# Attention sums of the last 14 row blocks in four column-group passes instead of two, with plain sums in the GRU state

## The chip, the cores and the metric

The kernel runs on one core of a Trainium2 chip as one launch. Its time is the device time of that launch in microseconds (us). The engines of the core work side by side and wait for each other by semaphores: TensorE (PE, matrix products; its weight loads are listed as PEld), VectorE (DVE), ScalarE (ACT, functions such as sigmoid and tanh), GpSimd (POOL), and SyncE (SP), which only issues transfers (DMA). A matrix product reads on-chip memory (SBUF) and writes one of eight banks of the accumulation memory (PSUM), where it can be added to what is there; the other engines read the banks.

## The reference, cut to what matters

The program is a graph network of four layers on 3327 nodes with 64 features each. Each layer is `x = x + L(relu(layernorm(x)), adj)`, with `adj` a matrix of 3327 x 3327 zeros and ones (about 0.5% ones). Layers 0 and 3 are hyperbolic attention layers; layer 1 is a decayed sum over neighbours. The change lies in layer 2:

```python
def gru_cell(x, h, w_ih, w_hh, b_ih, b_hh):
    gi = x @ w_ih.T + b_ih
    gh = h @ w_hh.T + b_hh
    ir, iz, inn = jnp.split(gi, 3, axis=1)
    hr, hz, hn = jnp.split(gh, 3, axis=1)
    r = jax.nn.sigmoid(ir + hr)
    z = jax.nn.sigmoid(iz + hz)
    n = jnp.tanh(inn + r * hn)
    return (1.0 - z) * n + z * h
...
A_node = node_adj - jnp.diag(d_node)
A_edge = edge_adj - jnp.diag(d_edge)
node_support = jnp.concatenate([(A_node > 0).astype(h.dtype) @ h, (A_node < 0).astype(h.dtype) @ h], axis=1)
edge_output = gru_cell(node_support, h, w_ih_e, w_hh_e, b_ih_e, b_hh_e)
edge_support = gat(h, A_node, A_edge, W_gat, a_gat)
node_output = gru_cell(edge_support, h, w_ih_n, w_hh_n, b_ih_n, b_hh_n)
return d_edge[:, None] * edge_output + d_node[:, None] * node_output
```

Since no entry of `adj` is negative, and all entries that count are one, every softmax in `gat` is the same over a row's neighbours: the attention is their mean. So layer 2 needs one product, the sum of h over each node's neighbours without the node itself (`A @ h`), and from it two GRU cells: g = 0 with the sum as its input, g = 1 with the mean (sum divided by degree) times W_gat. Only nodes with an entry on the diagonal of `adj` use the result.

## The kernel before, in words

**Layout.** The 3328 (padded) nodes are 26 row blocks of 128 (T = 26). Layer 2 works transposed: features on the 128 partitions, nodes along the columns; partitions 0 to 63 hold the features of the first 1664 nodes (half o = 0), partitions 64 to 127 those of the other half (HP = 1664). The columns of a half are C = 4 groups of BK = 416[...]. `masks` holds the whole adjacency as 8-bit ones and zeros with a cleared diagonal, `parts` the layer's h as a sum of two 16-bit halves.

**Sums.** `block(n, ks)` (L1761) adds row block n into the banks of the column groups ks: 2 parts x 2 halves = 4 matmuls per group (L1767). Group k's sum lies in bank k. Banks 0 and 1 are one PSUM tile, as are 2 and 3, 4 and 5, 6 and 7; a reader of one bank of a tile is ordered by the framework's tracking of tiles. The main loop (L1847) runs blocks 3 to 25; blocks up to 11 (`FULL` = 12) do all four groups, 16 matmuls, and blocks 12 to 25 only groups 0 and 1, 8 matmuls. Groups 2 and 3 of blocks 12 to 25 are done later.

**Small work inside the main loop.** `todo` (L1843) hangs work behind some blocks: `degrees` (L1779) corrects the degree of one column group by the diagonal (matmuls L1775, subtraction L1781); `inverse` (L1831) takes 1/degree by logarithm and exponential on ScalarE (L1834, L1835, L1836), and then loads ScalarE's table for sigmoid and tanh (L132); `inverse2` (L1839) refines it by two DVE operations over all 1664 columns; `weights2` (L1803) transposes W_gat and copies it (`wgT`), `weights3` (L1808) multiplies it into the weights of cell 1 (matmul L1811, copy L1812); `turn` (L1814) transposes up to four blocks of h (L1819) and makes five copies (on ACT L1827, on DVE L1825) into `hP` and the lower or upper half of the four tiles `xh[g][o]`.

**Eight steps.** A step (g, k) is one GRU cell on one column group. For each: `take` (L1869) copies the group's sum from its bank into xh[0] (ACT), `mean` (L1878) makes the mean from the bank and 1/degree (DVE), `take2` (L1882) copies that into xh[1] (ACT); `products` (L1887) are 16 matmuls into four banks (L1894 for r and z, 8 in all; L1899 for the two parts of n, 8); `sigmoids` (L1901) makes the two gates on ACT; `before_tanh` (L1909) combines the n parts on DVE (L1914, L1915); `tanh` (L1917) is on ACT; `state` (L1920) combines on DVE into `oP`, three operations for g = 0 and four for g = 1, which adds to the result of g = 0. The loop L1964 to the end is software pipelined by one step: in turn u come products(u), sigmoids(u), tanh(u−1), before_tanh(u), take2, state(u−1). Each engine has its own queue and runs its instructions in exactly this order; an instruction that waits holds up all behind it on its engine.

The order of steps is (0,0), (0,1), (1,0), (1,1), then (0,2), (0,3), (1,2), (1,3). The sums of groups 2 and 3 for blocks 12 to 25 stand between: 4, 3, 3, 3 and 1 blocks of 8 matmuls ahead of products(0) to products(4). Then the takes and means of groups 2 and 3. The four banks of products rotate over three pairs of banks (`RING`, L1861).

**The end of the stage.** The result goes back to node-major layout by transposes on PE (`turned`, L1943), and `use` (L1938) multiplies by the diagonal and adds to X on DVE (L1940, L1941). Tiles 0 to 5 go by plain transposes (L1271, in `from_pairs`). For tiles 6 to 12 the last two steps (1,2) and (1,3) don't add into `oP`: they leave two summands in two side tiles (`to_sum`; `state` L1926, L1927, cleared by GpSimd at L1867 where a tile of 128 crosses the group's edge), and PE adds the three terms by three matmuls with the identity per tile in PSUM (L1951). `last` is called at u = 6 (tiles 0 to 5), 7 (6 to 8) and 8 (9 to 12). Behind it layer 3 begins with the layernorm's reduction over the whole X (L434).

Of the kernel before, what the change touches and what calls it, by code (L numbers as in the profile page):

```python
# [10 lines left out]
F32 = mybir.dt.float32  # L11
# [10 lines left out]
P = 128  # L22
# [26 lines left out]
def tile_gnn4(ctx: ExitStack, tc: tile.TileContext, x, adjT, att0, b0, w1, bias1, w_gat, a_gat,  # L49
# [1694 lines left out]
    def plain_gat(masks, zo, deg, first, wg, gru, H, parts, banks, last_x, finish, close):  # L1744
# [9 lines left out]
        with ExitStack() as st:  # L1754
# [24 lines left out]
            def degrees(k, to):  # L1779
                cs = slice(k * BK, (k + 1) * BK)  # L1780
                V.tensor_sub(deg[:, cs], deg[:, cs], diagonal(k, to))  # L1781
# [18 lines left out]
            for _ in range(1):  # L1800
# [38 lines left out]
                def inverse2():  # L1839
                    V.scalar_tensor_tensor(deg, deg, -1.0, r0, op0=OP.mult, op1=OP.mult)  # L1840
                    V.scalar_tensor_tensor(deg, deg, 2.0, r0, op0=OP.add, op1=OP.mult)

                todo = {3: lambda: (degrees(2, 4), weights2(6)), 10: lambda: (degrees(3, 5), inverse()),  # L1843
                        12: lambda: turn(0, 6), 16: lambda: (inverse2(), turn(4, 4, V)),
                        22: lambda: weights3(7), 23: lambda: turn(8, 6), 25: lambda: turn(12, 5)}
                V.tensor_scalar(zo[:, 2 * T:2 * T + 2], zo[:, 2 * T:2 * T + 2], first, None, op0=OP.mult)
                for n in range(3, T):  # L1847
                    block(n, range(C) if n < FULL else range(C // 2))
                    if n in todo:
                        todo[n]()  # L1850
# [6 lines left out]
                halves = range(C // 2), range(C // 2, C)  # L1857
                steps = [(g, k) for ks in halves for g in range(2) for k in ks]
                K = len(steps)
                pg, gates, nns = {}, {}, {}  # L1860
                RING = 2, 3, 0  # L1861
                groups = range(0, 4), range(4, 6), range(6, 9), range(9, C2)
                c6 = groups[2].start * P
                summed = [(1, k) for k in halves[1]]
                to_sum = [tp.tile([P, HP - c6], F32, name=f"sum{i}") for i in range(2)]
                for t in to_sum:
                    G.memset(t[:, :C // 2 * BK - c6], 0.0)  # L1867

# [18 lines left out]
                def products(u):  # L1887
                    g, k = steps[u]
                    cs = slice(k * BK, (k + 1) * BK)
                    wx = gru[g][0]  # L1890
                    pg[u] = pr, pz, ph, pi = [bank(2 * RING[(2 * u + i // 2) % 3] + i % 2)[:, :BK] for i in range(4)]
                    for i, to in enumerate((pr, pz)):
                        for o in range(2):
                            PE.matmul(to[o * D:(o + 1) * D, :], wx[:, i, :], xh[g][o][:, cs], start=True, stop=True)  # L1894
                    for o in range(2):

                        for to, q in ((pi, o), (ph, 1 - o)):
                            r = slice(0, D) if to is pi else slice(D, P)
                            PE.matmul(to[q * D:(q + 1) * D, :], wx[r, 2, :], xh[g][q][r, cs], start=True, stop=True)  # L1899
# [9 lines left out]
                def before_tanh(u):  # L1909
                    bt = gru[steps[u][0]][1]  # L1910
                    g, k = steps[u]
                    nn = nns[u] = (to_sum[0][:, k * BK - c6:(k + 1) * BK - c6] if (g, k) in summed else
                                   tp.tile([P, BK], F32, name="nn", bufs=3))
# [6 lines left out]
                def state(u):  # L1920
# [3 lines left out]
                    if (g, k) in summed:  # L1924
                        o = to_sum[1][:, k * BK - c6:(k + 1) * BK - c6]
                        V.tensor_sub(o, hP[:, cs], nn)  # L1926
                        V.tensor_mul(o, o, gates[u][1])  # L1927
                        return
# [14 lines left out]
                def turned(i):  # L1943
                    pt = banks[2 + i % 2].rearrange("p (t h d) -> p t h d", h=2, d=D)
                    if i < 2:
                        from_pairs(None, oP, lambda *a: None, None, groups[i], pt)
                    else:
                        for k, t in enumerate(groups[i]):
                            for j in range(3):
                                src = oP[:, t * P:(t + 1) * P] if j == 0 else to_sum[j - 1][:, t * P - c6:(t + 1) * P - c6]  # L1950
                                PE.matmul(pt[:, k, :, :], src, ident, start=j == 0, stop=j == 2)  # L1951
                    return pt[:, :len(groups[i])].rearrange("p t h d -> p h t d")

                def last(*i):
                    for i, pt in [(i, turned(i)) for i in i]:
                        use(groups[i].start, len(groups[i]), pt)

                def takes(ks):
                    take(ks[0])
                    for k in ks:  # L1960
                        mean(k)
                    take(ks[1])

                blocks = iter(range(FULL, T))  # L1964
                between = {0: 4, 1: 3, 2: 3, 3: 3, 4: 1}
                takes(halves[0])
                for u in range(K + 2):
                    for _ in range(between.get(u, 0)):
                        block(next(blocks), halves[1])
                    if u == 4:  # L1970
                        takes(halves[1])
# [11 lines left out]
                    last(*{6: (0, 1), 7: (2,), 8: (3,)}.get(u, ()))  # L1983
# [103 lines left out]
```

## Time and profile before

| | |
|---|---|
| three timed executions | 731.65, 735.44, 739.38 us (median 735.44) |
| profiled execution | 731.25 us, span 729.4 us, mean granted TensorE clock 0.964 |
| busy share of the span | PE 87%, PEld 36%, DVE 74%, ACT 73%, POOL 59% |
| layer 2's sums and cells, up to L434's start | 380.8 to 466.8 us: 86.0 us |
| of it the main loop, up to the first products | 380.8 to 418.4 us |
| the eight steps' products | 418.4 to 449.0 us |
| the rest of the stage | 449.0 to 466.8 us |
| layer 3 | 466.8 to 729.4 us |

How to read it: all times are from one execution, counted from the start of its span. A row of the timeline has start, duration, engine, line of the source, operation, output and input by the program's names, shape and type, count of instructions in the row, and in brackets the engine's idle time before it with what ended it. The windows give each engine's busy time in a stretch, the number of its instructions, and the clock that TensorE was granted (1.00 is full). Matrix products are pipelined: a single one is listed with the time it takes from start to end, though the next begins earlier; the length of a stream is read from the starts.

### The profile page before, as it was taken

To read this page: it belongs to the slowest core of one execution; us is meant where nothing else is said; L and a number is where in the kernel's file an instruction comes from. 1 tells how busy PE (TensorE), PEld (TensorE's weight loads), DVE (VectorE), ACT (ScalarE), POOL (GpSimd) and SP (SyncE) were. 2 spreads that over 40 slices of the span, in tenths; PEclk is the share of its full clock that TensorE was granted. 3 is DMA by queue.
4 is the path that set the end of the run, shared out by engine and by line. 5 is a ranking of instruction groups with operands and counts; after the bars stand their busy time and mean duration, and the time that the engine had idled before them with its cause. 6 is when DMAs were issued, how large, how long until landed. Compare 5 with 4: busy or idle time off the path is not lost.

```text
span 729.4 us, 12038 instructions
## 1 busy us (share of the span) xinstructions
PE 638.0 (87%) x4262; PEld 261.9 (36%) x4262; DVE 541.9 (74%) x998; ACT 534.3 (73%) x688; POOL 430.0 (59%) x328
## 2 busy tenths in 40 slices
PE   0799999999999798989999996469999999999940
PEld 0522233333333233444446542442223333333310
DVE  6867777777777799999645458596667877777756
ACT  2788888888888785777861855258888889888831
POOL 2699989999999102017520000048887787888820
PEclk9999999999999999999999998569999999999985
DMA  3998888998888716489930000203334344433001
GB/s 63 325 280 277 265 276 257 284 289 269 265 262 270 254 56 224 134 290 359 402 130 2 1 1 1 93 18 94 95 93 133 107 118 144 119 118 118 2 2 50
DMA packets 61494, 119.25 MB, mean 164 GB/s; under 512 B 9552, under 2 KB 33776, under 8 KB 61424
## 3 DMA queue, kind: packets, MB, share of 16 engines
q1 hardware_dynamic: 57072, 118.38, 50.3%
q10 hardware_dynamic: 4352, 0.02, 0.3%
q8 instruction: 35, 0.57, 0.3%
q14 instruction: 35, 0.29, 0.1%
HBM read 115.64 MB, written 0.88 MB: 160 GB/s over the span
## 4 chain that ended last, share of the span: by engine, by line
PE 62%; DVE 13%; ACT 9%; issue 5%; POOL 5%; DMA 3%; ACTq 1%; SPq 0%; POOLq 0%; DVEq 0%
PE slot L630 16%; PE slot L638 9%; PE slot L611 9%; PE slot L1467 8%; PE slot L612 7%; PE slot L1481 5%; POOL sig L600 5%; PE slot L1767 3%; DMA adj<-in 3%; ACT sig L598 2%; PE slot L1894 1%; ACT slot L617 1%; PE slot L1951 1%; DVE X L1520 1%; ACTq L307 1%
## 5 line engine op out<-in xcount | busy, mean ns | idle before, releaser
L621 DVE SCALAR_TENSOR_TENSOR sig<-slot,sig 128x768 f32<-128x768 f32 (+1 forms) x208 | 212.5, 1022 | 106.4 <-POOL sig L600 106.1
L617 ACT ACTIVATE slot<-slot 128x768 f32<-128x768 f32 (+1 forms) x208 | 177.2, 852 | 54.1 <-PE slot L612 53.9
L600 POOL TENSOR_TENSOR sig<-adj,sig 128x768 f32<-128x768 f32 (+1 forms) x104 | 201.2, 1960 | 13.6 <-ACT sig L598 8.8
L598 ACT ACTIVATE sig<-leftB,right 128x768 f32<-128x768 f32 (+1 forms) x208 | 203.1, 977 | 0.1
L600 POOL TENSOR_TENSOR sig<-mask,sig 128x768 f32<-128x768 fp8e4 (+1 forms) x104 | 173.3, 1679 | 40.3 <-ACT sig L598 35.0
L630 PE MATMUL slot<-sig,Xr 128*64 128x384 f32 (+1 forms) x832 | 169.5, 526 | 6.3 <-DVE sig L621 6.1
L611 PE MATMUL slot<-XC,XT 128*128 128x384 f16 (+1 forms) x416 | 142.2, 342 | 2.9 <-ACT sum L648 1.7
L612 PE MATMUL slot<-XF,XE 73*128 73x384 f16 (+1 forms) x416 | 141.4, 340 | 0.0
L638 PE MATMUL slot<-sig,X 128*32 128x384 f32 (+1 forms) x832 | 94.2, 525 | 0.0
L1473 ACT ACTIVATE w<-slot,ebias 128x832 bf16<-128x832 f32 x76 | 69.0, 951 | 26.3 <-PE slot L1467 25.9
L630 PEld LDWEIGHTS slot<-sig,Xr 128*64 128x64 f32 x832 | 49.7, 135 | 87.9 <-issue 61.8
L611 PEld LDWEIGHTS <-XT 128*128 128x128 f16 x416 | 40.6, 98 | 93.8 <-issue 67.4
L1467 PE MATMUL slot<-mask,rest 128*128 128x416 fp8e4 x208 | 53.9, 341 | 5.7 <-ACT adj L1473 3.5
L1467 PE MATMUL slot<-mask,after 128*128 128x416 fp8e4 x208 | 53.4, 339 | 1.3 <-DVE deg L1491 1.3
L612 PEld LDWEIGHTS <-XE 73*128 73x128 f16 x416 | 40.7, 98 | 29.3 <-issue 5.1
L1362 DVE TENSOR_SCALAR_CACHE_REDUCE same<-late 128x832 fp8e4<-128x832 f32 x48 | 48.4, 1008 | 0.0
L204 POOL TENSOR_TENSOR mask<-mask,offdiag 128x128 fp8e4<-128x128 fp8e4 x26 | 15.4, 603 | 47.4 <-PE slot L1467 46.1
L638 PEld LDWEIGHTS slot<-sig,X 128*32 128x32 f32 x832 | 16.4, 108 | 67.7 <-issue 66.1
L1767 PE MATMUL slot<-mask,own 128*64 128x416 fp8e4 x416 | 39.4, 340 | 0.4 <-DVE deg L1491 0.4
L527 PE MATMUL pt<-ident_h,Xp 128*64 128x128 f16 x32 | 2.6, 314 | 36.1 <-ACT Xp L466 36.1
L1481 PE MATMUL slot<-w,h 128*64 128x416 bf16 x304 | 34.0, 345 | 0.0
L1512 POOL TENSOR_TENSOR X<-X,bias 128x256 f32<-128x256 f32 (+1 forms) x7 | 5.3, 785 | 46.1 <-DVE Xr L1527 46.1
(334 smaller groups left out, 690.6 us busy)
## 6 DMA issues: line engine op xcount, KB each, us to landing
adj<-in SPq DMA_DIRECT2D x78, 384.0 KB, 4.4
late<-in SPq DMA_DIRECT2D x48, 416.0 KB, 3.2
adj<-in SPq DMA_DIRECT2D x17, 832.0 KB, 8.0
adj<-in SPq DMA_DIRECT2D x27, 512.0 KB, 5.1
ahead<-in SPq DMA_DIRECT2D x14, 832.0 KB, 5.9
ahead<-in SPq DMA_DIRECT2D x16, 416.0 KB, 4.8
own<-in SPq DMA_DIRECT2D x16, 416.0 KB
own<-in SPq DMA_DIRECT2D x8, 832.0 KB
```

The costliest lines, as they stand in the source:

```text
L598: A.activation(sig, leftB[c], AF.Sigmoid, bias=right[:, b:b + 1])
L600: G.tensor_tensor(sig, adj, sig, op=OP.mult)
L611: PE.matmul(L[:, o, :c[1] * P], XT[:, rows], XC[c][:, o, :], start=True, stop=False)
L612: PE.matmul(L[:, o, :c[1] * P], XE[:KE, rows], XF[c][:, o, :], start=False, stop=True)
L617: A.activation(L, L, AF.Arctan, scale=PA / SX ** 2)
L621: V.scalar_tensor_tensor(sig, slot[:, :, :tiles[k][0][1] * P], PC, sig, op0=OP.add, op1=OP.mult)
L630: PE.matmul(acc[c][o * D:(o + 1) * D, 0, :n], Xr[:, b, :], sigs[k][:, o, :], start=b == 0, stop=b == T - 1)
L638: PE.matmul(acc[c][q:q + 32, 1, :n], X0[:, b - 1 + i, :], w[:, o, :], start=b == 1, stop=b == T - 1, tile_position=(0, q))
L1467: PE.matmul(cnt[o][:, h, :BK], w, cols(k, o, h), start=w is after and steps[k][1] == T - 1, stop=True, skip_group_check=True)
L1473: A.activation(ws[k][:, o, :, :], cnt[o][:, :, :BK], AF.Exp, scale=-LN2, bias=ebias)
L1481: PE.matmul(acc[c][o * D:(o + 1) * D, h, :BK], parts[i][:, b, :], w[:, o, h, :], start=b == T - 1 and i == 0, stop=b == 0 and i == 1)
L1767: PE.matmul(acc[k][o * D:(o + 1) * D, :], w, mask[:, o * HP + k * BK:o * HP + (k + 1) * BK], start=n == 0 and i == 0, stop=n == T - 1 and ...
```

## The change

The main loop's blocks 12 to 25 do group 0 alone (4 matmuls). The steps are ordered by group: (0,0), (1,0), (0,1), (1,1), (0,2), (1,2), (0,3), (1,3). Ahead of products(u), for u = 0 to 5, seven of the blocks 12 to 25 (the even ones at even u, the odd ones at odd u) are done for group u//2 + 1, 28 matmuls; so group 1 is summed during the two steps of group 0, group 2 during those of group 1, group 3 during those of group 2. At even u follow the take and the mean of group u//2. The side tiles, their memsets and the three-term sums are gone: every state adds into `oP`, and every tile goes back by a plain transpose, in groups of 3, 3, 3 and 4 tiles at u = 3, 5, 7 and 8, by way of banks 0 and 1. Products use banks 4 to 7 in every step but u = 6, which uses 2, 3, 0 and 1. In the main loop, turn(0), degrees(3) with inverse, weights2, inverse2 (now in two halves of 832 columns), weights3 and turn(8) hang behind other blocks; turn(12) stands in step 0 behind the take.

```diff
--- before.py
+++ after.py
@@ -1836,16 +1836,17 @@
                     A.activation(r0, r0, AF.Exp, scale=-1.0)
                     table_of(AF.Sigmoid, r0[:, :1])
-                def inverse2():
-                    V.scalar_tensor_tensor(deg, deg, -1.0, r0, op0=OP.mult, op1=OP.mult)
-                    V.scalar_tensor_tensor(deg, deg, 2.0, r0, op0=OP.add, op1=OP.mult)
-
-                todo = {3: lambda: (degrees(2, 4), weights2(6)), 10: lambda: (degrees(3, 5), inverse()),
-                        12: lambda: turn(0, 6), 16: lambda: (inverse2(), turn(4, 4, V)),
-                        22: lambda: weights3(7), 23: lambda: turn(8, 6), 25: lambda: turn(12, 5)}
+                def inverse2(c):
+                    d, r = [t[:, c * CW:(c + 1) * CW] for t in (deg, r0)]
+                    V.scalar_tensor_tensor(d, d, -1.0, r, op0=OP.mult, op1=OP.mult)
+                    V.scalar_tensor_tensor(d, d, 2.0, r, op0=OP.add, op1=OP.mult)
+
+                todo = {3: lambda: (degrees(2, 4), turn(0, 6)), 9: lambda: (degrees(3, 5), inverse()),
+                        11: lambda: weights2(7), 14: lambda: inverse2(0), 16: lambda: turn(4, 4, V),
+                        19: lambda: (weights3(6), inverse2(1)), 21: lambda: turn(8, 7)}
                 V.tensor_scalar(zo[:, 2 * T:2 * T + 2], zo[:, 2 * T:2 * T + 2], first, None, op0=OP.mult)
                 for n in range(3, T):
-                    block(n, range(C) if n < FULL else range(C // 2))
+                    block(n, range(C if n < FULL else 1))
                     if n in todo:
                         todo[n]()
@@ -1854,18 +1855,9 @@
-                halves = range(C // 2), range(C // 2, C)
-                steps = [(g, k) for ks in halves for g in range(2) for k in ks]
+                steps = [(g, k) for k in range(C) for g in range(2)]
                 K = len(steps)
                 pg, gates, nns = {}, {}, {}
-                RING = 2, 3, 0
-                groups = range(0, 4), range(4, 6), range(6, 9), range(9, C2)
-                c6 = groups[2].start * P
-                summed = [(1, k) for k in halves[1]]
-                to_sum = [tp.tile([P, HP - c6], F32, name=f"sum{i}") for i in range(2)]
-                for t in to_sum:
-                    G.memset(t[:, :C // 2 * BK - c6], 0.0)
-
                 def take(k, on=A):
                     cs = slice(k * BK, (k + 1) * BK)
                     for o in range(2):
@@ -1888,7 +1880,7 @@
                     g, k = steps[u]
                     cs = slice(k * BK, (k + 1) * BK)
                     wx = gru[g][0]
-                    pg[u] = pr, pz, ph, pi = [bank(2 * RING[(2 * u + i // 2) % 3] + i % 2)[:, :BK] for i in range(4)]
+                    pg[u] = pr, pz, ph, pi = [bank(i)[:, :BK] for i in ((2, 3, 0, 1) if u == K - 2 else range(4, 8))]
                     for i, to in enumerate((pr, pz)):
                         for o in range(2):
                             PE.matmul(to[o * D:(o + 1) * D, :], wx[:, i, :], xh[g][o][:, cs], start=True, stop=True)
@@ -1908,9 +1900,7 @@
                 def before_tanh(u):
                     bt = gru[steps[u][0]][1]
-                    g, k = steps[u]
-                    nn = nns[u] = (to_sum[0][:, k * BK - c6:(k + 1) * BK - c6] if (g, k) in summed else
-                                   tp.tile([P, BK], F32, name="nn", bufs=3))
+                    nn = nns[u] = tp.tile([P, BK], F32, name="nn", bufs=3)
                     V.scalar_tensor_tensor(nn, pg[u][2], bt[:, 5:6], gates[u][0], op0=OP.add, op1=OP.mult)
                     V.tensor_add(nn, nn, pg[u][3])
@@ -1921,11 +1911,6 @@
                     g, k = steps[u]
                     cs = slice(k * BK, (k + 1) * BK)
                     nn = nns[u]
-                    if (g, k) in summed:
-                        o = to_sum[1][:, k * BK - c6:(k + 1) * BK - c6]
-                        V.tensor_sub(o, hP[:, cs], nn)
-                        V.tensor_mul(o, o, gates[u][1])
-                        return
                     o = tp.tile([P, BK], F32, name="o", bufs=1)
                     V.tensor_sub(o, hP[:, cs], nn)
                     if g == 1:
@@ -1940,35 +1925,22 @@
                     V.tensor_mul(o[:, :, :n, :], src, d2[:, :, t0:t0 + n, None].to_broadcast([P, 2, n, D]))
                     V.tensor_add(X2[:, :, t0:t0 + n, :], X2[:, :, t0:t0 + n, :], o[:, :, :n, :])
-                def turned(i):
-                    pt = banks[2 + i % 2].rearrange("p (t h d) -> p t h d", h=2, d=D)
-                    if i < 2:
-                        from_pairs(None, oP, lambda *a: None, None, groups[i], pt)
-                    else:
-                        for k, t in enumerate(groups[i]):
-                            for j in range(3):
-                                src = oP[:, t * P:(t + 1) * P] if j == 0 else to_sum[j - 1][:, t * P - c6:(t + 1) * P - c6]
-                                PE.matmul(pt[:, k, :, :], src, ident, start=j == 0, stop=j == 2)
-                    return pt[:, :len(groups[i])].rearrange("p t h d -> p h t d")
-
-                def last(*i):
-                    for i, pt in [(i, turned(i)) for i in i]:
-                        use(groups[i].start, len(groups[i]), pt)
-
-                def takes(ks):
-                    take(ks[0])
-                    for k in ks:
-                        mean(k)
-                    take(ks[1])
-
-                blocks = iter(range(FULL, T))
-                between = {0: 4, 1: 3, 2: 3, 3: 3, 4: 1}
-                takes(halves[0])
+                groups = range(0, 3), range(3, 6), range(6, 9), range(9, C2)
+
+                def last(i):
+                    from_pairs(None, oP, use, None, groups[i],
+                               banks[i % 2].rearrange("p (t h d) -> p t h d", h=2, d=D))
+
                 for u in range(K + 2):
-                    for _ in range(between.get(u, 0)):
-                        block(next(blocks), halves[1])
-                    if u == 4:
-                        takes(halves[1])
+                    k = u // 2 + 1
+                    for n in range(FULL, T):
+                        if k < C and n % 2 == u % 2:
+                            block(n, range(k, k + 1))
+                    if u % 2 == 0 and u < K:
+                        take(u // 2)
+                        mean(u // 2)
+                    if u == 0:
+                        turn(12, 7)
                     if u < K:
                         products(u)
                         sigmoids(u)
@@ -1980,7 +1952,8 @@
                         take2(steps[u][1])
                     if 0 <= u - 1 < K:
                         state(u - 1)
-                    last(*{6: (0, 1), 7: (2,), 8: (3,)}.get(u, ()))
+                    if u in (3, 5, 7, 8):
+                        last((3, 5, 7, 8).index(u))
     def load():
         for ts in HALVES:
```

## The prediction, made before the result was known

> **What bounds the stage now.** I read the windows by stage first, then TensorE's timeline, then those of VectorE and ScalarE where TensorE waits. The windows (columns: stretch; its length; busy time and count on PE, PEld, DVE, ACT, POOL; granted clock; DMA share; GB/s):
>
> ```profile
> 380.80:418.40 37.60, 36.35 (x377) 22.28 (x375) 20.88 (x32) 17.90 (x32) 0.30 (x2) 1.00 0.01 2
> 418.40:449.00 30.60, 29.17 (x214) 11.85 (x214) 20.09 (x36) 19.10 (x37) 1.36 (x5) 1.00 0.00 1
> 449.00:466.80 17.80, 10.12 (x43) 9.08 (x42) 9.50 (x18) 1.53 (x3) 0.00 (x0) 0.62 0.28 95
> ```
>
> Up to 449 us PE is 95 to 97% busy: filling idle time there can win little. The 17.8 us behind it have half a PE and half a DVE, at a clock of 0.62. What those 17.8 us are, TensorE's timeline shows:
>
> ```profile
> 406.50 4.41 PE L1767 MATMUL slot<-mask,own 128*64 128x416 fp8e4 x48
> 411.41 0.54 PE L1811 MATMUL slot<-gw,wgT 64*64 64x192 f32 x2 [0.51 <-ACT xh L1827]
> ...
> 418.39 2.15 PE L1894 MATMUL slot<-xh,gw 128*64 128x416 f32 x8 [0.31 <-ACT xh L1874]
> 420.47 0.93 PE L1899 MATMUL slot<-xh,gw 64*64 64x416 f32 x8
> 421.33 2.30 PE L1767 MATMUL slot<-mask,own 128*64 128x416 fp8e4 x24
> 423.46 1.56 PE L1894 MATMUL slot<-xh,gw 128*64 128x416 f32 x8
> ...
> 440.12 2.15 PE L1894 MATMUL slot<-xh,gw 128*64 128x416 f32 x8 [0.83 <-ACT xh L1874]
> ...
> 448.07 0.93 PE L1899 MATMUL slot<-xh,gw 64*64 64x416 f32 x8
> 452.38 0.80 PE L1951 MATMUL slot<-ident,own 128*128 128x128 f32 x2 [3.38 <-DVE x L1940]
> ...
> 455.24 0.77 PE L1951 MATMUL slot<-ident,sum 128*128 128x128 f32 x2 [1.64 <-DVE sum L1927]
> ...
> 460.94 0.80 PE L1951 MATMUL slot<-ident,sum 128*128 128x128 f32 x2 [0.50 <-DVE sum L1927]
> ```
>
> Three things are to be seen. Steady streams: 24 sums (L1767) are followed 2.13 us later by the next products, so one costs 0.089 us; a step's 16 products last 2.35 us, or 2.93 when a fresh take (L1874) must finish halfway. PE then idles 3.38 us for DVE. And the identity sums of L1951 go in rows of 14 and 20 (455.24 to 458.58 and 460.94 to 465.3), 0.22 us each, with VectorE behind them:
>
> ```profile
> 458.61 0.56 DVE L1940 TENSOR_TENSOR x<-slot,dcol 128x384 f32<-128x384 f32 x1 [3.51 <-PE slot L1951]
> 465.33 0.69 DVE L1940 TENSOR_TENSOR x<-slot,dcol 128x512 f32<-128x512 f32 x1 [4.44 <-PE slot L1951]
> 466.78 1.95 DVE L434 TENSOR_REDUCE mean<-X 128x13 f32<-128x832 f32 x2
> ```
>
> Layer 3's layernorm (L434) reads the whole of X, so the last of these sets its start: the stage's end is 466.78, and I carry any change there to the end of the program.
>
> **What the Trainium skill says.** "TensorE: Matmul & The Clock Gate", section "What's actually happening": PE runs at half clock unless it was active over a free-running window of 3.41 us. The trace agrees: the granted clock is 1.0 until 451.21, 0.5 until 464.86 (four such windows), 1.0 again after a window of unbroken identity sums. The window that lost it, 447.79 to 451.21, had PE busy for 1.2 us (36%); one at 454.6 with 83% did not restore it; an idle of 1.89 us at 273.06 cost nothing. "PSUM — Partial Sum Buffer", section on bank collisions: a PE write and another engine's read of one bank must be kept apart. Before has a wait of that kind, ScalarE's take for VectorE's mean (2.79 us at 439.56). "VectorE: DVE Perf Modes", section on the TRN2 errata: an fp32 operation of n columns costs (n+151)/0.96 ns, so 0.59 us at 416; the trace has 0.58 to 0.59.
>
> **The change, part by part.**
>
> *Main loop.* Blocks 12 to 25 do 4 sums instead of 8: 56 matmuls leave it, 5.0 us. It doesn't win 5.0. degrees(3) moves one block earlier but behind turn(0,6)'s transposes (0.59), and a transpose of wg leaves its front (0.17): its matmul at 400.01 − 1.43 + 0.59 − 0.17 = 399.0. The chain behind it, fixed, is this:
>
> ```profile
> 402.07 1.68 ACT L1834 ACTIVATE few<-deg,hundred 128x1664 f32<-128x1664 f32 x1 [6.41 <-DVE deg L1833]
> ...
> 406.97 1.28 ACT L132 ACT_TABLE_LOAD   x1
> ...
> 408.37 0.58 ACT L1827 ACTIVATE hP<-slot 128x512 f32<-128x512 f32 x1
> ```
>
> It ends 8.36 us after that matmul, at 407.36. wgT's copy, moved from block 3 to block 11, is queued on ScalarE behind all of it; with 0.2 for the copy, 407.56. L1811 (block 19) needs wgT. PE gets there at 399.0 + 0.17 + 2.86 (two full blocks) + 0.17 + 2.86 (eight short blocks) + 0.59 (turn(4)) = 405.65 and waits 1.95 us, with all later sums behind it; before it waited 0.51 for its bank. From 407.6 on: L1811 0.47, two blocks 0.71, turn(8) 0.59, four blocks 1.43, the pass of 28 sums 2.50: 413.3. take(0), which shares a two-bank tile with group 1 and so waits for that pass's end, begins at 413.6. Products(0) start at 414.2, 4.2 us earlier than 418.39. turn(0,6)'s five ScalarE copies (2.98) go into ScalarE's 6.41 us of idle time ahead of L1834; were that cover gone, 2.98 would be added to the chain. The halved inverse2 (832 columns: 1.02 by the skill's formula instead of 1.89, twice each) has DVE idle around it: nothing. turn(12,7)'s five copies (0.28 + 1.12 in before) stand on ScalarE behind take(0) and end near 416.05; products(0)'s second half reads them and is due at 416.3: nothing, with 0.25 of cover, and up to 0.6 if the take starts late.
>
> *Eight steps.* 140 sums are left instead of 80: 5.4 us more. Starts: P1 = 414.2 + 2.93 + 2.50 = 419.6; P2, P3 4.85 each: 429.3; step 4: 429.3 + 2.35 + 0.45 (the three transposes of use(0), from the row of six in 0.80 at 445.72) + 2.50 = 434.6, and then take(2)'s first half, which waits for that pass (0.9, as take(0) did): P4 = 435.5; P5 = 435.5 + 2.93 + 2.50 = 440.9. Before: 440.12. So the weave brings nothing up to here (−4.2 + 5.4 − smaller waits = +0.8).
>
> *Tail.* P5 ends at 443.3, with transposes 443.75. DVE: before_tanh(5) to 444.75, state(4) 1.75 to 446.5, use(1) 1.1 to 447.6, mean(3) 0.56 to 448.1. products(6) goes to banks 2, 3, 0, 1 and mean(3) reads bank 3: a new wait. Queued behind it on PE are steps 6 and 7 and the last transposes; ScalarE's gates wait for those. P6 = 448.15, PE idle 4.4 us. Then, as the rows of before have it (gates 1.10 from P+1.61, tanh 0.64, take2 1.11, L1914 + L1915 1.25): take2(3) ends at 452.4, P7 begins 451.9, before_tanh(7) 454.75 to 456.0, state(6) to 457.8, use(2) 458.9, state(7), four adds, 2.35: 461.2. Four plain transposes to 461.9, use(3) 1.4: 463.35. Against 466.78 that is −3.4. The gain is L1951's: 3.34 + 4.37 = 7.7 us in the chain go, 1.1 of transposes come, and two more adds on the last state (1.2), the later P5 (0.8) and the wait for mean(3) take part of it back.
>
> *The clock.* That holds for a warm PE. An idle of 4.4 us always leaves one window with 2.2 us or more idle, as much as the one that lost the clock. So products(6) likely run at half clock: 4.5 instead of 2.35, and before_tanh(6), state(5) shift by 2.1; before_tanh(7) had 0.5 of slack behind them, so 1.6 reaches the end. Step 6 alone: −3.4 + 1.6 = −1.8. POOL's two memsets (L1867) go; they end long before. No DMA moves on SP's or POOL's queue, and layer 3's late loads follow state(7) as before.
>
> **Sum.** The profiled execution took 731.25 us (span 729.4), below the median 735.44. Forecast against it: −1.8, 729.45. On the scale of all four executions, whose middle is 733.5: 731.7.
>
> **Rivals.**
> *PE stays warm* (two short idles, or windows falling well): −3.4, 730.1. For it: the 1.89 us idle that cost nothing. Against: 4.4 is longer than the 3.38 that cost the clock.
> *Slower: the clock is lost twice.* The wait at L1811 is 1.95 us, like the 1.89 that did no harm, but before it the stream is not unbroken; if it drops, one window of 3.41 us at half speed costs 1.7. And if products(6) lose the clock, it may not be back before the end, as 13.65 us in before were not: step 7 and the last transposes cold as well put 2.2 more on the path (1.55 and 0.65): +0.4 instead of −1.8. Together +2.1: 735.6. It turns slower when step 7 is cold too. For it: 83% busy did not restore the clock, and step 7's stretch is no fuller.
> *Lockstep on four banks.* Before rotates three pairs; now steps 0 to 5 and 7 all use banks 4 to 7, so the second half of products(u+1) waits for before_tanh(u). That ends 3.8 us after P(u), and the half is due 6.3 after: 2.5 of slack. If DVE has a state of three operations (1.75) and more ahead, the slack goes at each of five steps: +8.8 on −1.8, 740.5. Against it: tanh and state sit behind before_tanh in program order.
> *Not doing what it says*: the program as built has 4-matmul blocks and 28-sum passes; nothing for it.
>
> **Numbers.** Forecast 0.42, warm 0.22, clock lost twice 0.28, lockstep 0.08. The range takes in the first three with the unknowns: L1811's wait (0.5 to 3), half a step of clock each way (1.7), and the spread between executions, which is 1% (that is also what a measurement here can tell): 727.5 to 737.5. Faster by over 1% (below 728.1) 0.12, slower by over 1% (above 742.8) 0.07, else within.
>
> **What would show it.** A wait at L1811 of about 2 us for ScalarE; products(0) near 414; PE idle of 4.4 us ahead of products(6), released by mean(3); a granted clock of 0.5 behind it; layer 3's first reduction near 465. Wrong it would be if products(6) didn't wait, if the passes' takes delay every even step by more than 0.9, or if layer 3 starts in another order so that its gain isn't carried.

## The result, and the profile after

| | before | after |
|---|---|---|
| timed executions, median | 733.87 us (20: 729.77 to 739.38) | 735.18 us (20: 731.61 to 737.75) |
| ratio after / before | | 1.0014, 95% interval 0.9995 to 1.0033 |
| profiled execution's span | 729.4 us | 731.5 us |
| first block sum (L1767) | 380.87 us | 382.68 us |
| layer 3's first reduction (L434) | 466.78 us | 467.35 us |
| the stage between these two | 85.91 us | 84.67 us |

The change makes no difference that this measurement can tell from zero: +1.0 us by the ratio, from −0.4 to +2.4. In this pair of profiles the stage itself is 1.24 us shorter. From here on "stage" is the time from the first block sum to L434, and times "in the stage" count from the first block sum, because layers 0 and 1, which the change doesn't touch, end up to 2.7 us apart from one execution to another.

The windows of the kernel after, in three parts (main loop; the first six steps; the rest with steps 6 and 7, while in the prediction's windows of before the second part holds all eight steps; columns as in the prediction):

```profile
382.60:416.10 33.50, 30.96 (x316) 19.01 (x314) 21.22 (x34) 16.62 (x27) 0.00 (x0) 1.00 0.01 2
416.10:445.60 29.50, 28.88 (x242) 13.22 (x242) 16.93 (x30) 15.57 (x33) 0.00 (x0) 1.00 0.00 1
445.60:467.35 21.75, 8.61 (x40) 3.03 (x39) 15.09 (x27) 6.24 (x12) 1.35 (x5) 0.83 0.15 51
```

The main loop has become 4.1 us shorter, and the part behind the last dense step longer: 21.75 us against 17.80, with TensorE busy for 8.6 and VectorE for 15.1. TensorE's timeline of after shows the waits (L1886 and L1891 are the products, L1894 and L1899 before; L1872 is the mean):

```profile
409.58 0.54 PE L1811 MATMUL slot<-gw,wgT 64*64 64x192 f32 x2 [1.78 <-ACT wgT L1806]
...
416.12 2.15 PE L1886 MATMUL slot<-xh,gw 128*64 128x416 f32 x8 [0.35 <-ACT xh L1866]
...
442.73 1.56 PE L1886 MATMUL slot<-xh,gw 128*64 128x416 f32 x8
...
445.08 0.55 PE L1271 MATMUL slot<-ident,own 128*128 128x128 f32 x3
449.93 3.04 PE L1886 MATMUL slot<-xh,gw 128*64 128x416 f32 x8 [4.30 <-DVE deg L1872]
...
455.14 2.19 PE L1886 MATMUL slot<-xh,gw 128*64 128x416 f32 x8 [1.27 <-ACT xh L1877]
...
464.75 1.12 PE L1271 MATMUL slot<-ident,own 128*128 128x128 f32 x4 [6.09 <-DVE own L1919]
```

The wait at L1811 is there, and the wait of products(6) for mean(3), 4.30 us, is the largest ahead of a step. (The 6.09 us ahead of the last transposes are a wait for the last state, with VectorE busy.) VectorE's timeline of after shows what mean(3) stood behind (L1925 and L1926 are `use`), and the end of the stage:

```profile
447.73 0.59 DVE L1919 TENSOR_TENSOR own<-o,nn 128x416 f32<-128x416 f32 x1
448.24 0.55 DVE L1925 TENSOR_TENSOR x<-slot,dcol 128x384 f32<-128x384 f32 x1
448.82 0.56 DVE L1926 TENSOR_TENSOR X<-X,x 128x384 f32<-128x384 f32 x1
449.30 0.58 DVE L1872 SCALAR_TENSOR_TENSOR deg<-slot,deg 128x416 f32<-128x416 f32 x1
454.05 0.65 DVE L1904 SCALAR_TENSOR_TENSOR nn<-slot,gb,gate 128x416 f32<-128x416 f32 x1 [4.17 <-PE slot L1891]
...
465.90 0.69 DVE L1925 TENSOR_TENSOR x<-slot,dcol 128x512 f32<-128x512 f32 x1 [1.21 <-PE slot L1271]
...
467.35 1.95 DVE L434 TENSOR_REDUCE mean<-X 128x13 f32<-128x832 f32 x2
```

VectorE's wait for the last returning tiles is 1.21 us, where it was 4.44 with the three-term sums: there lies the gain. Between its mean(3) and its next operation it idles for 4.17 us: there lies the loss. The experiments put a size to each.

### The profile page after: what moved, and what is told of

It is laid out like the page before. It is cut to its first block, busy times and chain, and to the rows that moved or that the text cites. A ratio compares the mean times of both kernels' runs of the same rounds, so it can differ in the third digit from the quotient of the medians.

```text
span 731.5 us, 11968 instructions
## 1 busy us (share of the span) xinstructions
PE 633.7 (87%) x4227; PEld 257.8 (35%) x4227; DVE 545.6 (75%) x1004; ACT 534.2 (73%) x688; POOL 432.3 (59%) x326
## 4 chain that ended last, share of the span: by engine, by line
PE 60%; DVE 12%; issue 7%; POOL 6%; ACT 6%; DMA 5%; SPq 2%; ACTq 1%; POOLq 0%; DVEq 0%
PE slot L630 15%; PE slot L1467 8%; PE slot L638 8%; PE slot L611 8%; PE slot L612 7%; POOL sig L600 6%; PE slot L1481 5%; PE slot L1767 4%; DMA adj<-in 4%; PE slot L1886 2%; ACT sig L598 2%; DVE sig L621 1%; DVE X L1520 1%; PE slot L1891 1%; ACT slot L617 1%
## 5 line engine op out<-in xcount | busy, mean ns | idle before, releaser
L421 POOL MEMSET X<- 128x832 f32 x2 | 1.6, 791 | 82.8 <-PE slot L1891 82.8
L204 POOL TENSOR_TENSOR mask<-mask,offdiag 128x128 fp8e4<-128x128 fp8e4 x26 | 17.3, 676 | 44.6 <-PE slot L1467 44.5
L1767 PE MATMUL slot<-mask,own 128*64 128x416 fp8e4 x416 | 39.4, 341 | 0.4 <-DVE deg L1491 0.4
```

The costliest lines, as they stand in the source:

```text
L1767: PE.matmul(acc[k][o * D:(o + 1) * D, :], w, mask[:, o * HP + k * BK:o * HP + (k + 1) * BK], start=n == 0 and i == 0, stop=n == T - 1 and ...
```

## The experiments

Each line of this table is one profiled execution; the ratio is that of the timed executions against the kernel before, run beside it. "P0", "P6", "P7" are the starts of the products of steps 0, 6 and 7 in the stage.

| kernel | P0 | P6 | P7 | stage | ratio, 95% interval |
|---|---|---|---|---|---|
| before | 37.52 | 62.19 | 65.66 | 85.91 | 1 |
| before, two more executions | 37.54, 37.53 | 62.21, 62.21 | 65.68, 65.68 | 85.53, 85.42 | |
| after | 33.44 | 67.25 | 72.46 | 84.67 | 1.0014 (0.9995 to 1.0033) |
| after, two more executions | 34.97, 33.44 | 68.79, 67.25 | 73.90, 71.97 | 86.11, 84.19 | |
| old order, plain sums | 37.54 | 62.21 | 65.68 | 82.46 | 0.9977 (0.9957 to 0.9998) |
| new order, three-term sums | 34.97 | 68.79 | 74.00 | 89.57 | 1.0005 (0.9985 to 1.0026) |
| after, mean(3) early | 33.45 | 62.90 | 67.04 | 79.72 | 0.9925 (0.9887 to 0.9963) |
| after, weights2 at block 3 | 40.83 | 74.65 | 79.22 | 91.43 | 1.0086 (1.0064 to 1.0107) |
| after, weights2 at block 9 | 32.41 | 66.23 | 70.77 | 82.98 | 0.9986 (0.9969 to 1.0003) |
| after, extra products into one half | 34.97 | 71.83 | 75.92 | 88.13 | 1.0015 (0.9992 to 1.0037) |
| after, extra products into both halves | 33.44 | 67.25 | 71.04 | 83.25 | |
| combined | 32.42 | 60.51 | 64.65 | 76.47 | 0.9861 (0.9835 to 0.9887) |

A profiled execution needn't be a typical one: that of the new order with three-term sums took 738.41 us, 3.2 above the median of its 20 timed executions, and that of weights2 at block 9, 728.83, is the fastest of its 20 and 4.5 below their median.

**One part of the change alone: plain sums in the old order.**

```diff
-                summed = [(1, k) for k in halves[1]]
-                to_sum = [tp.tile([P, HP - c6], F32, name=f"sum{i}") for i in range(2)]
...
+                summed = []
...
                 def turned(i):
...
-                    if i < 2:
-                        from_pairs(None, oP, lambda *a: None, None, groups[i], pt)
-                    else:
...
+                    from_pairs(None, oP, lambda *a: None, None, groups[i], pt)
```

> The kernel before with one part of the change alone: no side tiles, all states add into oP and all tiles go back by plain transposes; order of steps, sums and banks as before. Theory (the whole gain of the change lies in the three-term identity sums that go): VectorE has four more adds (2.4 us), the identity sums' 3.5 and 4.4 us of waiting shrink to about 1 each; stage 85.9 - 3.5 = 82.4, faster than both kernels (84.7 after). Rival (the gain comes from the weave): stage 85.5 to 87.

Measured: the stage is 82.46, 3.5 us less than in the first profile of before and 2.2 less than after. VectorE's timeline of this kernel (L1931 is the first operation of `use`):

```profile
459.20 0.56 DVE L1931 TENSOR_TENSOR x<-slot,dcol 128x384 f32<-128x384 f32 x1 [0.99 <-PE slot L1271]
...
463.82 0.69 DVE L1931 TENSOR_TENSOR x<-slot,dcol 128x512 f32<-128x512 f32 x1 [1.21 <-PE slot L1271]
...
465.27 1.94 DVE L434 TENSOR_REDUCE mean<-X 128x13 f32<-128x832 f32 x2
```

The two waits of 3.51 and 4.44 us before are 0.99 and 1.21, 5.75 us less, for four more adds of 0.59: that leaves 3.4, the gain of the stage. The timed executions show a smaller one, 1.7 us (0.1 to 3.2). So the plain sums alone gain more in the stage than the whole change does: the rest of it, taken together, loses 2.2 us there.

**The other part alone: the new order with three-term sums.**

```diff
                 pg, gates, nns = {}, {}, {}
+                c6 = 6 * P
+                summed = [(1, k) for k in range(C // 2, C)]
+                to_sum = [tp.tile([P, HP - c6], F32, name=f"sum{i}") for i in range(2)]
...
                 def last(i):
...
+                    for k, t in enumerate(groups[i]):
+                        for j in range(3):
+                            src = oP[:, t * P:(t + 1) * P] if j == 0 else to_sum[j - 1][:, t * P - c6:(t + 1) * P - c6]
+                            PE.matmul(pt[:, k, :, :], src, ident, start=j == 0, stop=j == 2)
```

> The kernel after with the three-term identity sums of before kept: steps (1,2) and (1,3) leave two summands in side tiles, and tiles 6 to 12 go back by three identity products each; the new order, passes and moved work stay. It is the part of the change that the plain sums are not. Theory (plain sums are the gain, the weave and its new wait are the loss): two adds less on the last state (1.2 us) but 24 identity products instead of 4 transposes behind it (4.4 us from state to use in before, 1.2 in after): stage 84.7 + 2.0 = 86.7 (86 to 88), slower than both kernels by 1 us or more. Rival (the plain sums bring nothing in the new order): stage 84 to 85.

Measured: 89.57 in the profile, of which 1.53 is a clock window lost ahead of P0 (34.97 against 33.44; see below), so 88.0, 3.4 above after. TensorE's and VectorE's timelines of this kernel (L1892 are products, L1912 is the first operation of before_tanh, L1938 of `use`):

```profile
456.61 3.61 PE L1892 MATMUL slot<-xh,gw 128*64 128x416 f32 x8 [0.57 <-ACT xh L1883]
```

```profile
461.55 0.65 DVE L1912 SCALAR_TENSOR_TENSOR sum<-slot,gb,gate 128x416 f32<-128x416 f32 x1 [2.95 <-PE slot L1897]
...
470.73 0.69 DVE L1938 TENSOR_TENSOR x<-slot,dcol 128x512 f32<-128x512 f32 x1 [3.96 <-PE slot L1951]
```

VectorE's wait for the last tiles is 3.96 us again. But not all of the 3.4 is the sums': in this execution the clock was at half from 450.63 to 460.87, through step 7 as well, where after had it back at 453.04. VectorE's before_tanh(7) starts 4.94 us behind P7 instead of 3.21, so 1.7 of the 3.4 are the clock's, and 1.6 are left for the three-term sums, near the theory's 2.0. The timed executions can't tell that: 1.0005 against after's 1.0014. As an end-to-end result it is inconclusive; the profile's direction is the theory's.

**The new wait taken away: mean(3) early.** After the pass of group 3, in step 5, its take and mean come at once; the mean has then been read when products(6) want its bank.

```diff
-                    if u % 2 == 0 and u < K:
-                        take(u // 2)
-                        mean(u // 2)
+                    if u in (0, 2, 4, 5):
+                        take((u + 1) // 2)
+                        mean((u + 1) // 2)
```

> The kernel after with take(3) and mean(3) issued behind group 3's pass in step 5, ahead of products(5), instead of in step 6. Stage = from the first block sum (L1767) to layer 3's first reduction (L434): 85.9 us in before, 84.7 in after. Theory (the new wait of products(6) for mean(3), which stands behind state(4) and use(1) on VectorE, is what the change pays): mean(3) fits into VectorE's idle time ahead of before_tanh(5), products(6) start about 0.1 us behind step 5's transposes with no idle of 4.3 us and at full clock, products(7) about 5.6 us earlier than in after, VectorE is then the bound of the tail; stage 79.2 (78.6 to 80). Rival (the tail is VectorE's queue anyway, the wait is hidden behind it): products(6) start earlier, the stage stays at 84 to 85.

Measured: P6 at 62.90 instead of 67.25, P7 at 67.04 instead of 72.46, stage 79.72: 5.0 us less than after; 79.2 were expected. The program is 0.75% faster than before (0.4 to 1.1). TensorE's and VectorE's timelines of this kernel:

```profile
446.22 1.62 PE L1886 MATMUL slot<-xh,gw 128*64 128x416 f32 x8
449.50 0.93 PE L1891 MATMUL slot<-xh,gw 64*64 64x416 f32 x8 [1.66 <-DVE x L1925]
```

```profile
444.68 0.59 DVE L1872 SCALAR_TENSOR_TENSOR deg<-slot,deg 128x416 f32<-128x416 f32 x1
445.95 0.65 DVE L1904 SCALAR_TENSOR_TENSOR nn<-slot,gb,gate 128x416 f32<-128x416 f32 x1 [0.68 <-PE slot L1891]
```

The mean lies in VectorE's idle time ahead of before_tanh(5), as expected. What takes the wait's place is smaller: the second half of products(6) goes to banks 0 and 1, from which use(1) reads the tiles that have come back (1.66 us). So the wait for mean(3), with what it brings on (the slower clock behind it among that), cost 5.0 us, more than the 2.2 by which the new order is behind the old one with plain sums.

**The wait at L1811.** Two versions. The first puts weights2 back to block 3, where before has it:

```diff
-                todo = {3: lambda: (degrees(2, 4), turn(0, 6)), 9: lambda: (degrees(3, 5), inverse()),
-                        11: lambda: weights2(7), 14: lambda: inverse2(0), 16: lambda: turn(4, 4, V),
+                todo = {3: lambda: (degrees(2, 4), weights2(7), turn(0, 6)), 9: lambda: (degrees(3, 5), inverse()),
+                        14: lambda: inverse2(0), 16: lambda: turn(4, 4, V),
```

> The kernel after with weights2 (transpose of wg and wgT's copy) back at block 3, ahead of degrees(3) and the ScalarE chain of the inverse. Theory (the 1.78 us that PE waits at the gw product are a second cost of the change and are passed on to all later sums): the wait at that product goes, products(0) come 1.7 us earlier after the first block sum, and the stage falls from 84.7 to 83.0. Rival (takes and ScalarE's copies of turn(8) then take its place): products(0) earlier by less than 0.7, stage 84.0 or more.

Measured: slower by 0.86%, a stage of 91.43. TensorE's timeline of it:

```profile
392.62 0.24 PE L1805 MATMUL slot<-ident,wg 64*64 64x64 f32 x1
398.37 1.11 PE L1819 MATMUL slot<-ident,own 128*128 128x128 f32 x4 [5.52 <-ACT wgT L1806]
399.42 10.98 PE L1767 MATMUL slot<-mask,own 128*64 128x416 fp8e4 x96
```

turn(0)'s transposes write bank 6, which is one tile with bank 7; so they wait until ScalarE has copied wgT out of bank 7, and ScalarE's copy is queued behind the layernorm's operations until 398.1. The idle time of 5.52 us also costs the clock: 96 sums take 10.98 us where they took 8.63. Theory and rival both missed it: they move the work ahead of a reader on ScalarE without looking at what is queued there. The second version puts it ahead of degrees(3), with ScalarE's copies of turn(0) done:

```diff
-                todo = {3: lambda: (degrees(2, 4), turn(0, 6)), 9: lambda: (degrees(3, 5), inverse()),
-                        11: lambda: weights2(7), 14: lambda: inverse2(0), 16: lambda: turn(4, 4, V),
+                todo = {3: lambda: (degrees(2, 4), turn(0, 6)), 9: lambda: (weights2(7), degrees(3, 5), inverse()),
+                        14: lambda: inverse2(0), 16: lambda: turn(4, 4, V),
```

> The kernel after with weights2 at block 9, just ahead of degrees(3), so that wgT's copy is queued on ScalarE behind turn(0)'s copies and ahead of the inverse's chain, and its bank 7 has no reader that is still to come. Theory: the wait of 1.78 us at the gw product goes, products(0) come 1.7 us earlier (31.7 instead of 33.4 behind the first block sum), stage 83.0; and PE has no idle time of 1.78 us there, in which a clock window can be lost (in the run with the extra matmuls that wait was followed by a window at 0.5 and products(0) were 1.5 later). Rival (ScalarE's turn(8) copies or VectorE's second half of inverse2 take the wait's place): products(0) at 32.7 or later.

Measured: products(0) at 32.41, 1.03 us earlier; the wait at L1811 is gone, but 0.76 of it comes back two rows later:

```profile
406.40 0.54 PE L1811 MATMUL slot<-gw,wgT 64*64 64x192 f32 x2
...
408.51 0.66 PE L1819 MATMUL slot<-ident,own 128*128 128x128 f32 x4 [0.76 <-ACT gw L1812]
```

gw's copy stands on ScalarE behind the table load, and turn(8) wants its tile. It lies between theory and rival. The stage is 1.7 less than after's first profile; the other 0.7 is that P7 follows P6 after 4.54 instead of 5.21, the clock having returned earlier. That part is chance: after itself has 5.21, 5.11 and 4.72 in its three profiles. The timed executions (0.9986, 0.9969 to 1.0003) don't tell the kernel from before.

**TensorE kept busy ahead of products(6).** 44 block sums that nobody reads, into a free bank:

```diff
+                    if u == K - 2:
+                        for i in range(44):
+                            PE.matmul(bank(4)[:D, :BK], parts[0][:, 0, 0, :], masks[0][:, 0, :BK], start=True, stop=True)
                     if u < K:
                         products(u)
```

> The kernel after with 44 extra matmuls of 128x416 in 8 bits on PE ahead of products(6), into bank 4, whose results nobody reads; they fill 3.9 of the 4.3 us in which PE waits for mean(3). Theory (half clock behind that idle time costs 1.5 us at the stage's end): products(6) start when they did, run in about 2.4 instead of 3.8 us at a granted clock of 1.0, stage 84.7 - 1.5 = 83.2. Rival (VectorE hides the slower products): products(6) fast, stage 84.4 to 84.9.

Measured: inconclusive for the clock. The extra products took 0.172 us each, so products(6) started 3.05 us late (after the same 1.53 ahead of P0), which hides what was to be measured. The second version writes the two halves of the bank in turn (`bank(4)[i % 2 * D:(i % 2 + 1) * D, :BK]`):

> As the run with 44 extra matmuls ahead of products(6), but they write the two halves of bank 4 in turn, as the block sums do, so that they should take 3.9 us (0.089 each) instead of the 7.4 that they took into one half (0.172 each), and not hold up products(6). Theory (half clock behind the idle time costs 1.1 to 1.5 us at the stage's end): products(6) where they were in after, 2.4 long, the time from there to layer 3's reduction 16.1 (17.4 in after). Rival: 17.0 or more.

Measured: products(6) where they were, 67.25, P7 at 71.04 instead of 72.46, and from P6 to layer 3's reduction 16.0 us instead of 17.4:

```profile
445.63 4.06 PE L1946 MATMUL slot<-mask,own 128*64 128x416 fp8e4 x44
450.00 1.62 PE L1886 MATMUL slot<-xh,gw 128*64 128x416 f32 x8 [0.31 <-DVE deg L1872]
```

So half clock behind the idle time cost 1.4 us at the end of the stage in after's first profile; in its two others the same stretch takes 17.3 and 16.9, which makes it 1.3 and 0.9. VectorE doesn't hide it: P7 and layer 3's reduction are later by the same 1.42.

**Further executions of both kernels**, since the pair of profiles and the timed executions differ in sign.

> The kernel before, unchanged, for another profiled execution. In the pair of profiles the stage is 1.2 us shorter after the change, in the timed executions the program is 1.0 us longer. Theory (what differs between executions is where the free-running clock window falls): the first products stand 37.5 us behind the first block sum as before, since nothing there waits long enough to lose the clock; only the tail of identity sums varies, stage 84 to 86. Rival (the stage is fixed and layers 0 or 3 got slower with the change): stage 85.7 to 86.1.

> The kernel after, unchanged, for another profiled execution. Theory (clock windows): products(0) at 33.4 behind the first block sum, or at 35.0 if the wait of 1.78 us at the gw product lies within one window, as in two of five profiles that have that wait; stage 84.7 or 86.2, and 1 us less if step 7 gets its clock back earlier. Rival: stage 84.5 to 84.9.

> As the other further execution of the kernel before: theory stage 84 to 86 with products(0) at 37.5; rival 85.7 to 86.1.

> As the other further execution of the kernel after: theory products(0) at 33.4 or 35.0, stage 83.5 to 86.5; rival 84.5 to 84.9.

Measured: before 85.53 and 85.42, after 86.11 and 84.19, all four outside the rivals' ranges. Before varies by half a microsecond: P0 to P7 are the same to 0.02 us in all three, and only the row of identity sums gets its clock back at different times. After varies by 1.9, and one of its causes is the wait of 1.78 us at L1811, in the execution with 86.11 (windows of one clock period; then TensorE's timeline):

```profile
406.43:409.84 3.41, 1.63 (x17) 0.78 (x14) 1.96 (x2) 3.09 (x4) 0.00 (x0) 1.00 0.00 0
409.84:413.26 3.42, 3.42 (x18) 1.50 (x18) 3.35 (x6) 0.63 (x2) 0.00 (x0) 0.50 0.02 5
```

```profile
409.62 0.72 PE L1811 MATMUL slot<-gw,wgT 64*64 64x192 f32 x2 [1.78 <-ACT wgT L1806]
410.27 1.60 PE L1767 MATMUL slot<-mask,own 128*64 128x416 fp8e4 x8
```

The wait lies within one window, which is busy for 1.63 of 3.41 us, and the next window runs at half clock: eight sums take 1.60 instead of 0.89, and P0 is 1.53 late. Of the seven profiles that have this wait, three lost that window (those with P0 at 34.97 in the table), four did not; on average it costs 0.66 us.

**What beats both: the parts together.** take and mean directly behind each pass, weights2 at block 9, and the use of tiles 6 to 8 behind the last state, where it covers the last transposes.

```diff
+                todo = {3: lambda: (degrees(2, 4), turn(0, 6)), 9: lambda: (weights2(7), degrees(3, 5), inverse()),
...
+                later = []
...
-                    from_pairs(None, oP, use, None, groups[i],
-                               banks[i % 2].rearrange("p (t h d) -> p t h d", h=2, d=D))
+                    from_pairs(None, oP, use if i != 2 else lambda *x: later.append(x), None, groups[i],
+                               banks[(0, 1, 0, 2)[i]].rearrange("p (t h d) -> p t h d", h=2, d=D))
...
-                    if u % 2 == 0 and u < K:
-                        take(u // 2)
-                        mean(u // 2)
+                    if u in (0, 1, 3, 5):
+                        take((u + 1) // 2)
+                        mean((u + 1) // 2)
...
+                    if u == K:
+                        use(*later[0])
                     if u in (3, 5, 7, 8):
                         last((3, 5, 7, 8).index(u))
```

> The kernel after with all of: take(k) and mean(k) for k = 1, 2, 3 behind their own pass in steps 1, 3 and 5, ahead of that step's products; weights2 at block 9; use of tiles 6 to 8 behind state(7), so that it covers the last transposes, which go to bank 2. Theory (the costs add up since PE bounds the steps and VectorE the tail): 84.7 - 5.0 (mean(3)) - 1.7 (weights2) - 0.9 (take(2)) - 1.1 (use behind state(7)) = 76.0 us of stage (75.5 to 77.5), 9 us less than before. Rival (VectorE's queue swallows what PE gains): 78.5 or more.

Measured: stage 76.47, 724.54 us, 1.4% faster than before (1.1 to 1.65). The end of VectorE's timeline has no wait left:

```profile
455.84 0.59 DVE L1919 TENSOR_TENSOR own<-o,nn 128x416 f32<-128x416 f32 x1
456.35 0.55 DVE L1925 TENSOR_TENSOR x<-slot,dcol 128x384 f32<-128x384 f32 x1
...
457.65 0.69 DVE L1925 TENSOR_TENSOR x<-slot,dcol 128x512 f32<-128x512 f32 x1
...
459.10 1.95 DVE L434 TENSOR_REDUCE mean<-X 128x13 f32<-128x832 f32 x2
```

So the new order is better than the old one once the wait for mean(3) is out of it: with mean(3) early alone its stage, 79.72, is below the old order's with plain sums, 82.46, and the timed medians, taken side by side, are 729.07 and 731.85 us. An old order with its own small work moved about in the same way was not run.

## Why the prediction was right, and where it was off

The time lies in the range (735.18 in 727.5 to 737.5), and the likeliest class, no change within 1%, is the one that came. The shift that it put first, −1.8 us, did not: the timed executions have +1.0 (−0.4 to +2.4). By its steps:

- **Main loop and six steps: right.** Products(0) were put at 33.3 in the stage and came at 33.44, products(5) at 60.0 and came at 60.05, the wait at L1811 at 1.95 and it was 1.78. "The weave brings nothing up to here" holds: P5 is at 59.25 before.
- **The gain: the right place, too large.** "The gain is L1951's" is what the old order with plain sums shows, but it shows 3.5 us. The prediction's terms for it, 7.7 − 1.1 − 1.2, make 5.4; they count two more adds where four come.
- **The new wait: right, but its share is too small.** Products(6) were put at 67.3 behind mean(3) with an idle time of 4.4; they came at 67.25 behind 4.30. It is a write of TensorE held up for another engine's read of the bank, as in the section that the prediction quotes; the 2.79 us that it names from before are a wait between two readers. Its split leaves 1.2 us for this wait and 1.6 for the clock behind it; the run without the wait shows 5.0. And the new order, which the split has at +0.8 for the later P5, is worth −2.7 without the wait (79.72 against 82.46). These errors cancel nearly. The total doesn't rest on the split but on the list of starts, and that held: at full clock (extra products into both halves) the stage is 83.25, 2.7 less than before, where the list has 3.4.
- **The clock: the mis-sized term.** "Step 6 alone: −3.4 + 1.6 = −1.8." The half clock behind the idle time cost 0.9 to 1.4, a little less than these 1.6 (2.1 less 0.5 of slack; the slack wasn't there). But the last four transposes, for which this case assumed full clock, take 1.12 us against 0.66 for four in the main loop: 0.46 more. And the rival's first half, a window lost behind L1811, priced at 1.7, came in three of seven profiles at 1.53. Its other half, a cold step 7, came in none of after's three. With −3.4 + 1.4 + 0.46 + 0.66 the sum is −0.9. The three profiles of each kernel have means of 85.0 and 85.6, −0.6.
- **Lockstep on four banks: didn't come.** Steps 2 and 3 follow their forerunners after 4.84 us, which is the 4.85 of the TensorE work alone.

One piece of evidence in the prediction was chance: the idle of 1.89 us at 273.06 "cost nothing" in that one execution. In the second execution of before the same idle of 1.89 us lies in a window with TensorE busy for 1.61 us, and the clock is lost behind it:

```profile
274.97:278.38 3.41, 1.61 (x12) 0.67 (x12) 3.27 (x6) 0.47 (x1) 0.00 (x0) 1.00 0.92 310
278.38:281.79 3.41, 3.41 (x16) 0.98 (x14) 3.27 (x18) 0.95 (x1) 0.00 (x0) 0.50 0.96 350
```

What stays open: the timed executions say +1.0 us (−0.4 to +2.4), the stage in the profiles −0.6. The old order with plain sums has such a gap too, −1.7 timed against −3.5 in the profile. In the three profiles of each kernel the whole span has become 0.8 us longer, close to the timed +1.0: −0.6 in the stage, +1.0 ahead of it and +0.5 behind it, where the change does nothing. Ahead of the stage, executions of both kernels scatter by 2.7 us. Behind it, from layer 3's first product to its first distance product there are 9.8 to 9.9 us or 11.1 to 11.3, depending on when the clock comes back: the longer time in two of three profiles of after and one of three of before, but over all fourteen profiles in three of ten of the new order and two of four of the old. So nothing shows that this goes systematically against the change; that it doesn't isn't shown either.

## What to carry to other kernels

When work is reordered to fill an engine, follow every reader of a buffer through the queue that it stands in: here a mean of 0.58 us, issued behind a state and a use on VectorE, held TensorE for 4.3 us and cost 5.0 us of the stage, and moving it up by one step in program order took the ratio to before from 1.0014 to 0.9925. Two buffers in one tile wait as one: the waits of 5.52 and 0.76 us in the runs that moved weights2 were for a bank's neighbour. And a stall of half a clock window is not only its own length, it can put the next 3.4 us of TensorE's work at half speed.

## What the runs showed of the hardware that I had not expected

- **The clock needs no wholly idle window to be lost.** The Trainium skill's "TensorE: Matmul & The Clock Gate", section "What's actually happening", has the slow state follow an idle window; here windows in which TensorE was busy for 1.63 of 3.41 us (48%, in three profiles) lost it, and windows with 1.71 (50%) and 1.92 (56%) kept it. One with 1.75 (51%) lost it. Of all windows at full clock between 255 and 500 us in the fourteen profiles, none busy for less than 1.57 us (46%) kept it and none busy for more than 1.75 lost it. So in these runs the border is near one half, and not sharp by the profile's busy time, in which the ends of products are modelled; a wait of 1.78 us is enough if it falls within one window.
- **How busy TensorE is doesn't tell when the clock comes back.** A window of products busy for 2.69 us (79%) restored it. Another of products with 2.84 (83%, steps 6 and 7 with three-term sums) didn't, nor did one of identity sums with 2.79 (82%), nor one of layer 3's transposes and small products with 3.37 (99%). What counts isn't shown.
- **Two products into the two halves of a bank cost little more than one.** 44 products of 128x416 with 64 output rows took 4.06 us in turn between the halves (output rows 0 to 63 and 64 to 127), 0.09 each, and 43 of them into one half 7.4 us, 0.172 each, both at a granted clock of 1.00. So the two of a pair ran side by side; the sums of a block, 0.089 each, alternate in the same way.
